# A macaron layer in split float32: the first block's norm and split ahead on VectorE, first loads in a new order, last tokens finished 128 at a time

## The chip, the cores and the metric

The kernel runs on one NeuronCore of a Trainium2 chip. A core has a matrix engine (TensorE, "PE" in the profile), a vector engine (VectorE, "DVE"), a scalar engine for activations and copies (ScalarE, "ACT"), a general engine (GpSimd, "POOL") and a queueing engine (SyncE, "SP"). Each runs its own list of instructions in order; semaphores tie them together. Transfers between main memory (HBM) and the on-chip memory (SBUF) are issued here from the SP queue and from the GpSimd queue; TensorE writes to eight banks of accumulation memory (PSUM).

The metric is the device time of one launch in microseconds (us). A profiled execution also leaves a trace, whose span runs from the first to the last instruction.

## What is computed

The input x has 4 sequences of 1024 positions with 256 features. Three residual steps follow one another:

```python
x = x + 0.5 * ffn(layernorm(x), ...)          # turn "f" in the kernel
x = x + attn(layernorm(x), ...)               # an S4D long convolution, "mix"
x = x + 0.5 * ffn(layernorm(x), ...)          # turn "g", same weights as "f"

def ffn(x, ...):                              # weights are -1, 0, 1; s is a scale per row
    h = silu(x @ w1.T * w1_s) * (x @ w2.T * w2_s)      # 256 -> 1024
    h = gelu(h @ h1.T * h1_s)                          # 1024 -> 1024
    h = gelu(h @ h2.T * h2_s)                          # 1024 -> 1024
    return h @ w3.T * w3_s                             # 1024 -> 256

def attn(x, ...):
    K = s4d_kernel(...)                       # 256 filters of 1024 taps
    y = irfft(rfft(x, 2048) * rfft(K, 2048))[:1024]
    return gelu(y) @ W.T + b
```

Everything is float32.

## The kernel before

The 4096 positions are cut into eight blocks of 512 (`TB`), each four tiles of 128 positions (`JT = 4`). The program goes through 16 turns in order: ("f", 0) to ("f", 7), then ("g", 0) to ("g", 7) (L771). One turn is one call of `ffn` (L247). The convolution of the four sequences (`mix`, L638), the computation of the filter's spectrum (`kernel_steps`, `kernel_spectrum`) and a check of the weights run beside the turns: a generator (`all_aside`, L794) is advanced one step at each `tick()` inside `ffn`.

An activation is kept as a pair: a high part rounded to a shorter float format ("fp32r") and a low part, the remainder (`low_part`, L217). A product with a ternary weight is then two matmuls of 128x128 by 128x512 into the same bank, one for each part (`linear`, L235).

In `ffn` there are eight output tiles m per layer. The gated layer takes 8 matmuls per m, four into `pa` (w1) and four into `pb` (w2): 64 in all. ScalarE makes silu(pa) (L258), VectorE multiplies by pb (L259), ScalarE casts the high part (L261), VectorE makes the low part (L217). Layers 2 and 3 take 16 matmuls per m, 128 per layer; ScalarE's gelu (L271) and cast (L273) and VectorE's remainder (L217) follow each m. The output layer (L289 to L312) works on two token tiles at a time: 32 matmuls of 256 columns into one bank (`po`), VectorE scales by 0.5 and w3_s (L303), GpSimd adds the residual (L311), and SP stores 256 KB (L312). The last call of the last turn ends the kernel, apart from a flag (`bad`, L836) that says whether every weight was held exactly; all engines read it at L844 and would run an unsplit version if it were set.

The input of the next turn is prepared during the current one (`prepare`, L774): its load (`load_x`, L166, three buffers `xb`), its norm (L198: statistics L204, their aggregation L206, the square root on ScalarE L207, then reciprocal L209 and normalisation L211 on VectorE), and its transposes on TensorE with the split of the result (`transposed`, L219). For block 0 the norm and transposes come ahead of the loop (L808 to L810).

The order of work on an engine is not written out: a scheduler orders all instructions by priority and by when it thinks that their operands are ready, and gives out buffers and semaphores. So an instruction of a later block may stand ahead of one of block 0 on the same engine, and once the list is fixed an engine waits at its head.

The first loads, in the order of the program (L178 to L195): SP takes x of block 0, the constants `cst`, the `scales`, x of block 1, the filter's parameters `k_in` (L187, L188), then `w3_s`, `wt` and `bias`; GpSimd's queue takes w1 and w2 in four pieces of 512 KB, h1 and h2 in eight pieces of 1 MB, and w3.

Of the kernel before, what the change touches and what calls it, by code (L numbers as in the profile page):

```python
# [2 lines left out]

# [1 line left out]

# [6 lines left out]
F32 = mybir.dt.float32  # L12
# [79 lines left out]
def macaron_layers(  # L92
# [34 lines left out]
    def bank(name):  # L127
        return psum.tile([P, 512], F32, tag="ps", name=name)
# [5 lines left out]
    def ring(name, *shape, dtype=F32):  # L134

        return work.tile([P, *shape], dtype, tag="ring", name=name, bufs=15)
# [23 lines left out]
    def column(i):  # L160
        return cst_sb[:, i : i + 1]

    def positions(t, b, j, n=2):
        return t[b].rearrange("(p j) d -> p j d", j=J)[:, j : j + n, :]

    def load_x(t, blk, name):  # L166
        b, g = divmod(blk, J // JT)
        xb = work.tile([P, JT, D], F32, tag="xb", name=name, bufs=3)
        nc.sync.dma_start(xb, positions(t, b, g * JT, JT))
        return xb  # L170

    def rows(w):
# [2 lines left out]

    weights_from = nc.gpsimd if split else nc.sync

    x_first = load_x(x, 0, "x_f0")  # L178
    nc.sync.dma_start(cst_sb[:, 0:C_N], cst)
    nc.sync.dma_start(sc_sb, scales)  # L180
    for k in range(DC):
        weights_from.dma_start(w1_sb[:, k, :], rows(w1)[:, k, :])
        weights_from.dma_start(w2_sb[:, k, :], rows(w2)[:, k, :])
    x_second = load_x(x, 1, "x_f1")
    k_in = half("k_in", 4, DD)
    k_in2 = half("k_in2", 4, DD)
    nc.sync.dma_start(k_in, kin[:, 0:4, :])  # L187
    nc.sync.dma_start(k_in2[:, 0, :], kin[:, 4, :])  # L188
    for t, src in ((h1_sb, h1), (h2_sb, h2)):
        for k in range(0, KH, 2):  # L190
            weights_from.dma_start(t[:, k : k + 2, :], rows(src)[:, k : k + 2, :])
# [3 lines left out]
    nc.sync.dma_start(bias_sb, bias.partition_broadcast(P))  # L195


    def norm(t, name):  # L198

        stats = small.tile([P, JT, 6], F32, tag="stats", name=f"stats_{name}")  # L200
        mv = small.tile([P, JT, 2], F32, tag="mv", name=f"mv_{name}")
        rstd = small.tile([P, JT], F32, tag="rstd", name=f"rstd_{name}")
        for i in range(JT):
            nc.vector.bn_stats(stats[:, i, :], t[:, i, :])  # L204
        for i in range(JT):
            nc.vector.bn_aggr(mv[:, i, :], stats[:, i, :])  # L206
        nc.scalar.activation(rstd, mv[:, :, 1], AF.Sqrt, bias=column(C_EPS))  # L207
        yield
        nc.vector.reciprocal(rstd, rstd)  # L209
        for i in range(JT):  # L210
            ts(t[:, i, :], t[:, i, :], mv[:, i, 0:1], rstd[:, i : i + 1], ALU.subtract, ALU.mult)  # L211
        yield


    def low_part(t, src):

        tt(t[:, 1, :], src, t[:, 0, :].bitcast(F32), ALU.subtract)  # L217

    def transposed(xn, name):  # L219

        xt = []
        for k in range(DC):
            pt = bank(f"pt_{name}_{k}")
            for i in range(JT):
                nc.tensor.transpose(  # L225
                    pt[:, i * P : (i + 1) * P], xn[:, i, k * P : (k + 1) * P], ident
                )
            t = ring(f"xt_{name}_{k}", parts, TB, dtype=wide)
            nc.vector.tensor_copy(t[:, 0, :], pt)  # L229
            if split:  # L230
                low_part(t, pt)
            xt.append(t)
        return xt

    def linear(ps, w, m, acts):  # L235
        n = len(acts)
# [7 lines left out]
                    stop=(k == n - 1 and part == parts - 1),  # L244
                )

    def ffn(xt, src, dst, blk, name, tick, ahead):  # L247

        ha = []
        for m in range(KH):
            pa, pb = bank(f"pa_{name}_{m}"), bank(f"pb_{name}_{m}")
            linear(pa, w1_sb, m, xt)
            linear(pb, w2_sb, m, xt)
            g = half(f"g_{name}_{m}")
            t = ring(f"ha_{name}_{m}", parts, TB, dtype=wide)
            nc.scalar.activation(g, pa, AF.Silu, scale=sc_sb[:, 0, m : m + 1])  # L258
            stt(g if split else t[:, 0, :], pb, sc_sb[:, 1, m : m + 1], g, ALU.mult, ALU.mult)  # L259
            if split:  # L260
                nc.scalar.copy(t[:, 0, :], g)  # L261
                low_part(t, g)
            ha.append(t)
        for layer, w in ((2, h1_sb), (3, h2_sb)):
            hb = []
            for m in range(KH):
                ps = bank(f"p{layer}_{name}_{m}")
                linear(ps, w, m, ha)
                t = ring(f"h{layer}_{name}_{m}", parts, TB, dtype=wide)
                g = half(f"g{layer}_{name}_{m}") if split else t[:, 0, :]  # L270
                nc.scalar.activation(g, ps, AF.Gelu, scale=sc_sb[:, layer, m : m + 1])  # L271
                if split:
                    nc.scalar.copy(t[:, 0, :], g)  # L273
                    low_part(t, g)
                hb.append(t)
                if layer == 3:
                    ahead()
                if m < KH - 1:
                    tick()
            ha = hb  # L280
        ahead(last=True)
        tick()
        b, g = divmod(blk, J // JT)
        rest = []
        for i in range(0, JT, 2):
            xr = half(f"xr_{name}_{i}", 2, D)
            nc.sync.dma_start(xr, positions(src, b, g * JT + i))
            rest.append(xr)
        for i in range(0, JT, 2):  # L289
            xr = rest[i // 2]  # L290
            ps = bank(f"po_{name}_{i}")
            for e in range(2):
                for k in range(KH):
                    for part in range(parts):
                        nc.tensor.matmul(  # L295
                            ps[:, e * D : (e + 1) * D],
                            ha[k][:, part, (i + e) * P : (i + e + 1) * P],
                            w3_sb[:, k, :],
                            start=(k == 0 and part == 0),
                            stop=(k == KH - 1 and part == parts - 1),  # L300
                        )
            y = half(f"y_{name}_{i}", 2, D)
            stt(  # L303
                y,
                ps.rearrange("p (e d) -> p e d", e=2),
                0.5,
                w3s_sb[:, None, :].to_broadcast([P, 2, D]),
                ALU.mult,
                ALU.mult,
            )  # L310
            nc.gpsimd.tensor_tensor(y, xr, y, ALU.add)  # L311
            nc.sync.dma_start(positions(dst, b, g * JT + i), y)  # L312

    def weight_checks():

# [489 lines left out]
            yield from weight_checks()  # L805

    aside = all_aside()
    for _ in norm(x_first, "f0"):  # L808
        pass
    xt = transposed(x_first, "f0")  # L810
    for n, (turn, blk) in enumerate(blocks):
        following = []
        steps = [prepare(*b, following) for b in blocks[n + 1 : n + 2]]

        def ahead(last=False):
            for step in steps:
                if last:
                    done.append(("last layer", *blocks[n + 1][::-1]))
                next(step, None)

        src, dst = (x, x1) if turn == "f" else (x2, out)
        ffn(xt, src, dst, blk, f"{turn}{blk}", lambda: next(aside, None), ahead)
        done.append((turn, blk))
        xt = following
    for _ in aside:
# [86 lines left out]
```

## Time and profile before

| | us |
|---|---|
| median of three executions | 1465.45 |
| lowest and highest | 1464.86 and 1466.04 |
| the profiled execution | 1466.05 |
| its span, first to last instruction | 1464.1 |
| VectorE busy in the span | 860.5 |
| ScalarE busy in the span | 666.1 |
| one matmul 128x512, mean of its modelled duration in layers 2 and 3 | 0.39 |
| one silu or gelu of 128x512 (L258, L271) | 0.69 |
| one cast of 128x512 on ScalarE (L273) | 0.62 |
| one remainder of 128x512 on VectorE (L217) | 0.69 |
| one product with the gate on VectorE (L259) | 0.75 |

The profile is read in steps. The page gives each engine's busy time and, in 40 slices, when it is busy. The chain of waits is followed back from the last instruction to whatever released it. The waits name, for an engine that stood idle, which instruction waited and what released it. The timeline lists instructions in order of start. Matmuls are pipelined and their ends are modelled, so their spacing (0.227 us in long rows, the chain's 240 matmuls in 54.42) says more than their duration. Idle time of an engine that isn't the one everything waits for costs nothing.

### The profile page before, as it was taken

To read this page: it belongs to the slowest core of one execution; us is meant where nothing else is said; L and a number is where in the kernel's file an instruction comes from. 1 tells how busy PE (TensorE), PEld (TensorE's weight loads), DVE (VectorE), ACT (ScalarE), POOL (GpSimd) and SP (SyncE) were. 2 spreads that over 40 slices of the span, in tenths; PEclk is the share of its full clock that TensorE was granted. 3 is DMA by queue.
4 is the path that set the end of the run, shared out by engine and by line. 5 is a ranking of instruction groups with operands and counts; after the bars stand their busy time and mean duration, and the time that the engine had idled before them with its cause. 6 is when DMAs were issued, how large, how long until landed. Compare 5 with 4: busy or idle time off the path is not lost.

```text
span 1464.1 us, 18076 instructions
## 1 busy us (share of the span) xinstructions
PE 1429.7 (98%) x7074; PEld 1213.7 (83%) x7074; DVE 860.5 (59%) x1616; ACT 666.1 (45%) x996; POOL 74.4 (5%) x71
## 2 busy tenths in 40 slices
PE   5999999999999999997999999999999999999997
PEld 4788888888888888886888888888888888888886
DVE  5776574765744634667367673676736667464521
ACT  3677353783534434442454344543445334353432
POOL 2000000000000000000100001000010000100000
PEclk9999999999999999999999999999999999999999
DMA  9110000100001111210312113121121111633000
GB/s 365 33 42 2 15 30 4 40 1 29 15 29 44 62 46 38 72 58 29 101 51 87 37 36 94 48 89 37 36 94 44 65 37 36 221 117 101 21 9 17
DMA packets 42975, 85.50 MB, mean 58 GB/s; under 512 B 4737, under 2 KB 9985, under 8 KB 42881
## 3 DMA queue, kind: packets, MB, share of 16 engines
q1 hardware_dynamic: 39088, 72.73, 15.1%
q0 software_dynamic: 3792, 11.54, 2.2%
q8 instruction: 57, 0.93, 0.3%
q14 instruction: 38, 0.30, 0.1%
HBM read 69.05 MB, written 15.20 MB: 58 GB/s over the span
## 4 chain that ended last, share of the span: by engine, by line
PE 94%; DMA 2%; DVE 2%; ACT 1%; issue 0%; POOL 0%; SPq 0%; POOLq 0%; DVEq 0%
PE p_f L239 32%; PE p_g L239 30%; PE po_f L295 4%; PE po_g L295 4%; PE pa_g L239 4%; PE pb_g L239 4%; PE pa_f L239 3%; PE pb_f L239 3%; PE pi L731 2%; PE pf_m L561 2%; PE pk L497 2%; PE pw L751 2%; DMA x_f<-in_x_dram 1%; DMA k_in<-in_kin_dram 1%; PE pt_f L225 1%; DVE given L328 1%
## 5 line engine op out<-in xcount | busy, mean ns | idle before, releaser
L239 PE MATMUL p_f<-ha_f,h_sb 128*128 128x512 f32 x1024 | 242.4, 394 | 1.8 <-ACT ha_f L261 0.9
L239 PE MATMUL p_f<-h_f,h_sb 128*128 128x512 f32 x1024 | 240.4, 392 | 0.0
L239 PE MATMUL p_g<-h_g,h_sb 128*128 128x512 f32 x1024 | 236.0, 390 | 0.0
L239 PE MATMUL p_g<-ha_g,h_sb 128*128 128x512 f32 x1024 | 234.5, 390 | 0.0
L239 PEld LDWEIGHTS p_f<-ha_f,h_sb 128*128 128x128 f32 x1024 | 192.2, 189 | 43.5 <-ACT ha_f L261 1.6
L239 PEld LDWEIGHTS p_g<-ha_g,h_sb 128*128 128x128 f32 x1024 | 192.2, 188 | 39.9
L239 PEld LDWEIGHTS p_g<-h_g,h_sb 128*128 128x128 f32 x1024 | 192.2, 188 | 39.8
L239 PEld LDWEIGHTS p_f<-h_f,h_sb 128*128 128x128 f32 x1024 | 190.9, 188 | 40.0 <-DVE h_f L217 0.3
L271 ACT ACTIVATE g_g<-p_g,sc_sb 128x512 f32<-128x512 f32 x128 | 88.2, 689 | 273.4 <-PE p_g L239 268.6
L217 DVE TENSOR_TENSOR h_f<-g_f,h_f 128x512 fp32r<-128x512 f32 x128 | 88.3, 691 | 193.0 <-ACT h_f L273 192.8
L271 ACT ACTIVATE g_f<-p_f,sc_sb 128x512 f32<-128x512 f32 x128 | 88.0, 688 | 245.6 <-PE p_f L239 245.3
L217 DVE TENSOR_TENSOR h_g<-g_g,h_g 128x512 fp32r<-128x512 f32 x128 | 88.4, 691 | 171.4 <-ACT h_g L273 171.1
L273 ACT CAST h_g<-g_g 128x512 fp32r<-128x512 f32 x128 | 79.4, 620 | 3.9
L273 ACT CAST h_f<-g_f 128x512 fp32r<-128x512 f32 x128 | 79.1, 619 | 3.4
L258 ACT ACTIVATE g_g<-pa_g,sc_sb 128x512 f32<-128x512 f32 x64 | 44.0, 687 | 66.5 <-PE pa_g L239 64.4
L239 PE MATMUL pa_f<-xt_f,w_sb 128*128 128x512 f32 x256 | 70.5, 395 | 1.8 <-DVE xt_f L229 1.2
L259 DVE SCALAR_TENSOR_TENSOR g_g<-pb_g,sc_sb,g_g 128x512 f32<-128x512 f32 x64 | 47.9, 748 | 37.2 <-PE pb_g L239 29.8
L239 PE MATMUL pb_f<-xt_f,w_sb 128*128 128x512 f32 x256 | 69.2, 392 | 0.0
L239 PE MATMUL pa_g<-xt_g,w_sb 128*128 128x512 f32 x256 | 68.6, 390 | 0.0
L239 PE MATMUL pb_g<-xt_g,w_sb 128*128 128x512 f32 x256 | 68.4, 389 | 0.0
L295 PE MATMUL po_g<-w_sb,h_g 128*128 128x256 f32 x512 | 64.2, 285 | 2.2 <-DVE h_g L217 2.2
L295 PEld LDWEIGHTS po_g<-w_sb,h_g 128*128 128x128 f32 x512 | 62.3, 192 | 2.9 <-DVE h_g L217 2.8
(216 smaller groups left out, 1682.3 us busy)
## 6 DMA issues: line engine op xcount, KB each, us to landing
h_sb<-in_h_dram POOLq DMA_DIRECT2D x8, 1024.0 KB, 22.6
given<-in_h_dram SPq DMA_DIRECT2D x32, 256.0 KB, 4.7
kr<-k_hat SPq DMA_DIRECT2D x20, 256.0 KB, 2.7
ki<-k_hat SPq DMA_DIRECT2D x20, 256.0 KB, 2.9
x_f<-in_x_dram SPq DMA_DIRECT2D x8, 512.0 KB, 3.8
xr_f<-in_x_dram SPq DMA_DIRECT2D x16, 256.0 KB, 3.5
x<-y_f SPq DMA_DIRECT2D x16, 256.0 KB, 2.4
xm<-x SPq DMA_DIRECT2D x8, 512.0 KB, 4.1
```

Source lines behind the costliest of these rows:

```text
L217: tt(t[:, 1, :], src, t[:, 0, :].bitcast(F32), ALU.subtract)
L225: nc.tensor.transpose(pt[:, i * P : (i + 1) * P], xn[:, i, k * P : (k + 1) * P], ident)
L239: nc.tensor.matmul(ps, w[:, k, m * P : (m + 1) * P], acts[k][:, part, :], start=(k == 0 and part == 0), stop=(k == n - 1 and part == parts ...
L258: nc.scalar.activation(g, pa, AF.Silu, scale=sc_sb[:, 0, m : m + 1])
L259: stt(g if split else t[:, 0, :], pb, sc_sb[:, 1, m : m + 1], g, ALU.mult, ALU.mult)
L271: nc.scalar.activation(g, ps, AF.Gelu, scale=sc_sb[:, layer, m : m + 1])
L273: nc.scalar.copy(t[:, 0, :], g)
L295: nc.tensor.matmul(ps[:, e * D : (e + 1) * D], ha[k][:, part, (i + e) * P : (i + e + 1) * P], w3_sb[:, k, :], start=(k == 0 and part == 0) ...
L497: nc.tensor.matmul(pk[:, at + i, :, :].rearrange("p h b -> p (h b)"), a[:, i].rearrange("p a b -> p (a b)"), qd[d1 // per_tile][:, at + i, ...
L561: nc.tensor.matmul(ps[e][:, part, :], m[:, e, part, :], rows_of(q + JQ * e), start=True, stop=True)
L731: nc.tensor.matmul(banks[dc][e][:, q * P : (q + 1) * P], vs[q + JQ * e][:, part, dc * P : (dc + 1) * P], m[:, e, part, :], start=(part == ...
L751: nc.tensor.matmul(ps[:, e * D : (e + 1) * D], yts[dc][j // JQ][:, (j % JQ + e) * P : (j % JQ + e + 1) * P], wt_sb[:, dc, :], start=(dc == 0),
```

## The change

Four edits, all in the split version that runs:

- Loads. Block 0's x is loaded as two transfers of two token tiles each. Block 1's x, `k_in` and `k_in2` move from SP's queue to GpSimd's queue, behind w1 and w2 and ahead of h1.
- Norm and transposes of block 0. `norm` takes `parts_of`: for block 0 (`parts_of=2`) statistics, root, reciprocal and normalisation are done for two token tiles at a time. `transposed` takes `first`: the transposes then go token tile by token tile over both banks, VectorE copies the high part of xt_0, ScalarE that of xt_1, and the two remainders follow on VectorE.
- Order. The whole first call of `ffn`, with all that is traced within it (the steps of `all_aside` and the preparation of block 1 among them), stands in a block `tc.issue_after(last_split.ins)`. It puts each VectorE instruction traced in it behind the last remainder of block 0's split on VectorE. It adds no wait of its own at run time; it fixes the order.
- Output. In the last turn (`final`), the last two token tiles get a bank each, 16 matmuls each; for each of them VectorE scales 128x256, VectorE and not GpSimd adds the residual, and SP stores 128 KB.

As the scheduler builds it, TensorE's list is unchanged but for the order of block 0's transposes and first products. VectorE's list begins with block 0's statistics, reciprocals and normalisations, one copy and two remainders; then come three of block 1's four statistics; then the eight gates of block 0 with their remainders and the product on k_in; then the norms of blocks 1, 2 and 3, mixed with the filter's computation and the remainders of layer 2. From about the 127th entry to the end of the last turn VectorE's list is the old one. ScalarE's table switches for the roots of blocks 1 to 3 stand behind block 0's gates instead of among them. On SP, the read of the flag follows the last store; before, it came ahead of it.

```diff
@@ -163,10 +163,10 @@
     def positions(t, b, j, n=2):
         return t[b].rearrange("(p j) d -> p j d", j=J)[:, j : j + n, :]
 
-    def load_x(t, blk, name):
+    def load_x(t, blk, name, queue=nc.sync):
         b, g = divmod(blk, J // JT)
         xb = work.tile([P, JT, D], F32, tag="xb", name=name, bufs=3)
-        nc.sync.dma_start(xb, positions(t, b, g * JT, JT))
+        queue.dma_start(xb, positions(t, b, g * JT, JT))
         return xb
 
     def rows(w):
@@ -175,17 +175,20 @@
 
     weights_from = nc.gpsimd if split else nc.sync
 
-    x_first = load_x(x, 0, "x_f0")
+    x_first = work.tile([P, JT, D], F32, tag="xb", name="x_f0", bufs=3)
+    for i in range(0, JT, 2):
+        nc.sync.dma_start(x_first[:, i : i + 2, :], positions(x, 0, i))
     nc.sync.dma_start(cst_sb[:, 0:C_N], cst)
     nc.sync.dma_start(sc_sb, scales)
     for k in range(DC):
         weights_from.dma_start(w1_sb[:, k, :], rows(w1)[:, k, :])
         weights_from.dma_start(w2_sb[:, k, :], rows(w2)[:, k, :])
-    x_second = load_x(x, 1, "x_f1")
+
+    x_second = load_x(x, 1, "x_f1", queue=weights_from)
     k_in = half("k_in", 4, DD)
     k_in2 = half("k_in2", 4, DD)
-    nc.sync.dma_start(k_in, kin[:, 0:4, :])
-    nc.sync.dma_start(k_in2[:, 0, :], kin[:, 4, :])
+    weights_from.dma_start(k_in, kin[:, 0:4, :])
+    weights_from.dma_start(k_in2[:, 0, :], kin[:, 4, :])
     for t, src in ((h1_sb, h1), (h2_sb, h2)):
         for k in range(0, KH, 2):
             weights_from.dma_start(t[:, k : k + 2, :], rows(src)[:, k : k + 2, :])
@@ -195,42 +198,60 @@
     nc.sync.dma_start(bias_sb, bias.partition_broadcast(P))
 
 
-    def norm(t, name):
+    def norm(t, name, parts_of=1):
 
         stats = small.tile([P, JT, 6], F32, tag="stats", name=f"stats_{name}")
         mv = small.tile([P, JT, 2], F32, tag="mv", name=f"mv_{name}")
         rstd = small.tile([P, JT], F32, tag="rstd", name=f"rstd_{name}")
-        for i in range(JT):
-            nc.vector.bn_stats(stats[:, i, :], t[:, i, :])
-        for i in range(JT):
-            nc.vector.bn_aggr(mv[:, i, :], stats[:, i, :])
-        nc.scalar.activation(rstd, mv[:, :, 1], AF.Sqrt, bias=column(C_EPS))
-        yield
-        nc.vector.reciprocal(rstd, rstd)
-        for i in range(JT):
-            ts(t[:, i, :], t[:, i, :], mv[:, i, 0:1], rstd[:, i : i + 1], ALU.subtract, ALU.mult)
+        step = JT // parts_of
+        for at in range(0, JT, step):
+            here = range(at, at + step)
+            for i in here:
+                nc.vector.bn_stats(stats[:, i, :], t[:, i, :])
+            for i in here:
+                nc.vector.bn_aggr(mv[:, i, :], stats[:, i, :])
+            nc.scalar.activation(
+                rstd[:, at : at + step], mv[:, at : at + step, 1], AF.Sqrt, bias=column(C_EPS)
+            )
+        yield
+        for at in range(0, JT, step):
+            nc.vector.reciprocal(rstd[:, at : at + step], rstd[:, at : at + step])
+            for i in range(at, at + step):
+                ts(
+                    t[:, i, :],
+                    t[:, i, :],
+                    mv[:, i, 0:1],
+                    rstd[:, i : i + 1],
+                    ALU.subtract,
+                    ALU.mult,
+                )
         yield
 
 
     def low_part(t, src):
 
-        tt(t[:, 1, :], src, t[:, 0, :].bitcast(F32), ALU.subtract)
-
-    def transposed(xn, name):
-
-        xt = []
+        return tt(t[:, 1, :], src, t[:, 0, :].bitcast(F32), ALU.subtract)
+
+    def transposed(xn, name, first=False):
+
+
+        pts = [bank(f"pt_{name}_{k}") for k in range(DC)]
+        order = [(k, i) for k in range(DC) for i in range(JT)]
+        for k, i in sorted(order, key=lambda o: o[1]) if first else order:
+            nc.tensor.transpose(
+                pts[k][:, i * P : (i + 1) * P], xn[:, i, k * P : (k + 1) * P], ident
+            )
+        xt = [ring(f"xt_{name}_{k}", parts, TB, dtype=wide) for k in range(DC)]
+        last = None
+        if first:
+            last = nc.vector.tensor_copy(xt[0][:, 0, :], pts[0])
+            nc.scalar.copy(xt[1][:, 0, :], pts[1])
         for k in range(DC):
-            pt = bank(f"pt_{name}_{k}")
-            for i in range(JT):
-                nc.tensor.transpose(
-                    pt[:, i * P : (i + 1) * P], xn[:, i, k * P : (k + 1) * P], ident
-                )
-            t = ring(f"xt_{name}_{k}", parts, TB, dtype=wide)
-            nc.vector.tensor_copy(t[:, 0, :], pt)
+            if not first:
+                nc.vector.tensor_copy(xt[k][:, 0, :], pts[k])
             if split:
-                low_part(t, pt)
-            xt.append(t)
-        return xt
+                last = low_part(xt[k], pts[k])
+        return (xt, last) if first else xt
 
     def linear(ps, w, m, acts):
         n = len(acts)
@@ -244,7 +265,7 @@
                     stop=(k == n - 1 and part == parts - 1),
                 )
 
-    def ffn(xt, src, dst, blk, name, tick, ahead):
+    def ffn(xt, src, dst, blk, name, tick, ahead, final):
 
 
 
@@ -286,10 +307,10 @@
             xr = half(f"xr_{name}_{i}", 2, D)
             nc.sync.dma_start(xr, positions(src, b, g * JT + i))
             rest.append(xr)
-        for i in range(0, JT, 2):
-            xr = rest[i // 2]
-            ps = bank(f"po_{name}_{i}")
-            for e in range(2):
+
+        def result(ps, i, n):
+
+            for e in range(n):
                 for k in range(KH):
                     for part in range(parts):
                         nc.tensor.matmul(
@@ -299,17 +320,37 @@
                             start=(k == 0 and part == 0),
                             stop=(k == KH - 1 and part == parts - 1),
                         )
-            y = half(f"y_{name}_{i}", 2, D)
+
+        def finish(ps, y, xr, i, n, add_on):
             stt(
                 y,
-                ps.rearrange("p (e d) -> p e d", e=2),
+                ps.rearrange("p (e d) -> p e d", e=n),
                 0.5,
-                w3s_sb[:, None, :].to_broadcast([P, 2, D]),
+                w3s_sb[:, None, :].to_broadcast([P, n, D]),
                 ALU.mult,
                 ALU.mult,
             )
-            nc.gpsimd.tensor_tensor(y, xr, y, ALU.add)
-            nc.sync.dma_start(positions(dst, b, g * JT + i), y)
+            add_on.tensor_tensor(y, xr, y, ALU.add)
+            nc.sync.dma_start(positions(dst, b, g * JT + i, n), y)
+
+        for i in range(0, JT, 2):
+            y = half(f"y_{name}_{i}", 2, D)
+            if final and i + 2 == JT:
+                for e in range(2):
+                    ps = bank(f"po_{name}_{i + e}")
+                    result(ps, i + e, 1)
+                    finish(
+                        ps[:, 0:D],
+                        y[:, e : e + 1, :],
+                        rest[i // 2][:, e : e + 1, :],
+                        i + e,
+                        1,
+                        nc.vector,
+                    )
+            else:
+                ps = bank(f"po_{name}_{i}")
+                result(ps, i, 2)
+                finish(ps, y, rest[i // 2], i, 2, nc.gpsimd)
 
     def weight_checks():
 
@@ -805,9 +846,9 @@
             yield from weight_checks()
 
     aside = all_aside()
-    for _ in norm(x_first, "f0"):
+    for _ in norm(x_first, "f0", parts_of=2):
         pass
-    xt = transposed(x_first, "f0")
+    xt, last_split = transposed(x_first, "f0", first=True)
     for n, (turn, blk) in enumerate(blocks):
         following = []
         steps = [prepare(*b, following) for b in blocks[n + 1 : n + 2]]
@@ -819,7 +860,8 @@
                 next(step, None)
 
         src, dst = (x, x1) if turn == "f" else (x2, out)
-        ffn(xt, src, dst, blk, f"{turn}{blk}", lambda: next(aside, None), ahead)
+        with tc.issue_after(last_split.ins) if n == 0 else nullcontext():
+            ffn(xt, src, dst, blk, f"{turn}{blk}", lambda: next(aside, None), ahead, n + 1 == len(blocks))
         done.append((turn, blk))
         xt = following
     for _ in aside:
```

More of the change, by code (lines that the diff above doesn't have):

```diff
@@ L1 @@
 import math
-from contextlib import ExitStack
+from contextlib import ExitStack, nullcontext
 import numpy as np
```

## The prediction

> **What bounds the kernel now.** I read the page first. TensorE is busy in 98% of the span, and in its 40 slices only the first and last, and two in the middle, are not full:
>
> ```profile
> PE 1429.7 (98%) x7074; PEld 1213.7 (83%) x7074; DVE 860.5 (59%) x1616; ACT 666.1 (45%) x996; POOL 74.4 (5%) x71
> PE   5999999999999999997999999999999999999997
> ```
>
> So a change can only gain where TensorE stands still. The waits of TensorE over the whole run say where that is; nearly all of it is the start and one place near 690 us:
>
> ```profile
> PE pt_f L225 <- DVE x_f L211: 13.8, 1, 13.8
> PE pi L731 <- DVE v_False L722: 7.4, 1, 7.4
> ```
>
> The change touches the first and leaves the second. The timeline of the first microseconds (start, duration, engine, line, operation, idle time before it and what ended it):
>
> ```profile
> 4.51 1.41 DVE L204 BATCH_NORM_STATS2 stats_f<-x_f 128x6 f32<-128x256 f32 x4 [3.63 <-DMA x_f<-in_x_dram]
> 4.74 1.28 ACT L207 ACT_TABLE_LOAD   x1 [4.74 <-DMA cst_sb<-in_cst_dram]
> 6.23 0.30 ACT L207 ACTIVATE rstd_f<-mv_f,cst_sb 128x4 f32<-128x4 f32 x1 [0.21 <-DVE mv_f L206]
> 10.89 1.08 DVE L204 BATCH_NORM_STATS2 stats_f<-x_f 128x6 f32<-128x256 f32 x3 [4.70 <-DMA x_f<-in_x_dram]
> 11.89 0.16 DVE L209 RECIPROCAL rstd_f<-rstd_f 128x4 f32<-128x4 f32 x1
> 12.96 0.29 DVE L413 TENSOR_SCALAR k_in<-k_in,cst_sb 128x128 f32<-128x128 f32 x1 [0.91 <-DMA k_in<-in_kin_dram]
> 13.16 1.46 DVE L211 TENSOR_SCALAR x_f<-x_f,mv_f,rstd_f 128x256 f32<-128x256 f32 x4
> 13.76 2.24 PE L225 MATMUL pt_f<-ident,x_f 128*128 128x128 f32 x8 [13.76 <-DVE x_f L211]
> 17.21 1.72 PE L239 MATMUL pa_f<-xt_f,w_sb 128*128 128x512 f32 x2 [1.20 <-DVE xt_f L229]
> 23.95 1.41 DVE L204 BATCH_NORM_STATS2 stats_f<-x_f 128x6 f32<-128x256 f32 x4 [4.36 <-DMA x_f<-in_x_dram]
> 38.96 0.50 PE L239 MATMUL p_f<-ha_f,h_sb 128*128 128x512 f32 x1 [0.22 <-DVE ha_f L217]
> ```
>
> Block 0's 1/std is ready at 6.53, but VectorE runs in order and the queue's next entries are block 1's statistics (their load lands at 10.89) and a product on k_in (lands about 12.9). So 1/std waits till 11.89 and the normalisation till 13.16. Later VectorE waits at 23.95 and 26.56 for the statistics of blocks 2 and 3, and ScalarE swaps tables for their roots, all while block 0's gates stand behind; TensorE starves between 35 and 40.35. Its clock then drops (stretches of time: busy PE, PEld, DVE, ACT, POOL; granted clock, DMA share, GB/s):
>
> ```profile
> 42.00:43.00 1.00, 1.00 (x4) 0.81 (x3) 0.97 (x4) 0.12 (x1) 0.00 (x0) 0.50 0.00 0
> 47.00:48.00 1.00, 1.00 (x7) 0.81 (x6) 0.00 (x0) 0.97 (x2) 0.00 (x0) 1.00 0.00 0
> ```
>
> The end: last products, then VectorE's scaling, GpSimd's addition, the store:
>
> ```profile
> 1448.41 8.09 PE L295 MATMUL po_g<-w_sb,h_g 128*128 128x256 f32 x64
> 1456.54 0.69 DVE L303 SCALAR_TENSOR_TENSOR y_g<-po_g,w3s_sb 128x512 f32<-128x512 f32 x1 [2.78 <-PE po_g L295]
> 1457.36 1.26 POOL L311 TENSOR_TENSOR y_g<-xr_g,y_g 128x512 f32<-128x512 f32 x1 [2.18 <-DVE bad L836]
> 1455.21 3.79 SPq L312 DMA_DIRECT2D out_dram<-y_g  x2
> ```
>
> [...] matmuls start 0.43 us apart from 18.72, and 0.227 us apart only after 21.0, 3.8 us after the first; the clock is 0.50 from 41.25 to 44.5. [...] against 4 KB packets of weights on GpSimd's queue, SP's 1 KB packets crawl (wt takes 14.9 us, bias 15.4), so block 2's load, issued at 6.62 behind them, lands at 23.95.
>
> **The change part by part.** Zero is the start of the profiled span.
>
> Block 0's norm. The load becomes two of 256 KB; cst is now third on SP, not second, one issue of 0.41 us later. ScalarE's table load waits for cst: 4.74 + 0.41 = 5.15, loaded at 6.4, first root (0.30) at 6.7. The statistics and aggregations, 1.41 + 0.36 = 1.8 us, fit before that unless a half lands after about 4.9, so the split load gains little: the table is the limit. Then two reciprocals (0.16) and four normalisations (0.35 apart), with gaps, 6.75 to 8.6. Transposes now go token tile by token tile, the last pair starts at 8.65 and ends at 9.3 (0.26 apart). Cast of xt_0 0.68: first matmul at 10.0 instead of 17.21. xt_1 is copied by ScalarE meanwhile (a 128x512 copy from PSUM takes 0.59 at L565), so the two remainders, 0.68 each, are done at 10.6 and 11.2; TensorE's first xt_1 product is its tenth. Bound: a half or cst landing 0.7 later moves all this by 0.7; earlier by at most 0.4, since only cst's extra issue was added.
>
> Weights. GpSimd's next issues show the four pieces of w1 and w2 landed by 8.27, 10.84, 12.87 and 14.48. The new order needs them at matmul 1, 2, 10 and 17: 10.0, 10.4, about 14.3 and 16. Even at the old landings only 0.4 is lost. SP now has one 512 KB load fewer before them, which makes them earlier; I take 0, range 0 to 0.8.
>
> Gates of block 0 (64 matmuls). Half rate at first: [...] I take 4.5, to 14.5, with 10 matmuls done. The other 54 take 0.2268 each (the chain has 240 in 54.42): 12.2, so they end at 26.7. VectorE: 8 x (0.75 + 0.69) = 11.5 us, ScalarE 8 x (0.69 + 0.62) = 10.5 us, both less than TensorE, as the built order puts only three statistics of block 1 ahead of the gates and the rest of blocks 1 to 3 behind. Block 1's load moves to GpSimd's queue, fifth, behind 2 MB of w1 and w2, and should land at 13 to 17. VectorE waits there with all gates behind it. The first gate then is ready 1.8 us later (three statistics, one 0.75), and TensorE needs its bank at matmul 41, at 21.3: a landing up to 19.5 costs nothing. The last remainder comes at about 29.7 even then; the built order reaches it as the 23rd matmul of the next layer, at 31.5.
>
> h1. Its first 1 MB landed by 17.7; x_f1 and k_in (0.84 MB) now go ahead: 2.1 us at 400 GB/s, so 19.8, then 2.6 us per MB to 27.7. Needed from 26.7, the last quarter after 20 matmuls, 31.2. No stall; margin 3 us.
>
> Layers 2 and 3. Before, TensorE reaches block 1's transposes at 97.41; 256 products at 0.2268 are 58.1, so full rate would have begun at 39.35. After: 26.7. Gain 12.65: 7.2 in the first matmul, 5.45 in stalls and the 1.7 us of half clock [...]. The moved norms (about 9 us of VectorE) land in block 0's layers 2 and 3, where VectorE has room: 59% over the run. From about VectorE's 127th entry all engines' orders match the old, and TensorE has no wait till 684.7, so the gain is carried through.
>
> End. Two banks, two halves. Scaling and addition of 128x256 take 0.42 each on VectorE (L703 shows that shape): 1456.43 + 0.11 + 0.42 + 0.05 + 0.42 = 1457.43, against 1458.62: gain 1.2. SP now reads the flag behind the last store instead of ahead of it: 0 to 0.8 lost; a store of half the size lands 0 to 0.3 sooner. I take 1.2, range 0.4 to 1.5.
>
> Sum: 12.65 + 1.2 = 13.85. The profiled execution took 1466.05 (span 1464.1 and 1.95 around it), so 1452.2; it is 0.6 above the median of 1465.45, so against that 1451.6.
>
> **The rivals.**
> Loads or a cold array hold the start: one of the late cases above each (cst or a half 0.7, weights 0.8, [...] h1 or bank waits 2), 4.6 together: 1456.2. For it: DMA is saturated until 40. Against: bytes ahead of w1, w2 shrank.
> Given back at 690: if VectorE's later work were a backlog, the 7.4 us wait at L731 grows by 12.65, and only the end gains: 1464.3, no measurable change. Against: VectorE last waited for ScalarE's cast at 686.14, which follows TensorE, so that wait is a local chain of about 5 us.
> Slower: block 1's load heads VectorE's queue ahead of every gate. If GpSimd's queue doesn't serve in order and x_f1 lands with the last loads, at about 39.5, TensorE stalls 39.5 - 19.5 = 20: 1471.6. It decides from a landing at 19.5 + 13.85 = 33.4. For it: x_f2 took 17.3 us from issue. Against: w1 and w2 landed in their order in 14.5 us.
> That the change fails to do what it says is excluded by the built order: block 0's norm is first on VectorE.
>
> **How the numbers follow.** Forecast 0.76; held start 0.15; given back 0.04; slower 0.03; and 0.02 for a start better by 3 (warm at once, weights and x early): 1448.6. The forecast's own spread is 1449.5 to 1454.5; with the held start, 1449.2 to 1456.5 holds 8 in 10 and somewhat more. This kernel's measurement tells 0.2%, 2.9 us, from no change. Faster 0.93, same 0.04, slower 0.03.
>
> **What would show it.** First matmul near 10 with block 0's reciprocal before any other block's statistics; no wait of TensorE for ha_f; block 1's transposes at 84.8; no half clock near 42; the L731 wait still near 7.4; VectorE's last addition about 1.0 us after the last matmul. Wrong would be: x_f1 landing after 19.5, TensorE waiting for w_sb or h_sb, or a second half-clock stretch in block 0.

## The result, and the profile after

| | before | after |
|---|---|---|
| median of six executions, us | 1465.38 | 1455.69 |
| lowest and highest | 1464.86 and 1466.04 | 1454.43 and 1457.52 |
| ratio to before, with its 95% interval | | 0.9936 [0.9923, 0.9948] |
| the profiled execution, and its span | 1466.05, 1464.1 | 1457.52, 1455.7 |

The change gains 9.7 us. The forecast of 1451.6 is 4.1 too low; the stated range, 1449.2 to 1456.5, holds the result. Where the time went is read from the timeline of the changed kernel's start (start, duration, engine, line, operation, idle time before it and what ended it):

```profile
3.97 0.75 DVE L210 BATCH_NORM_STATS2 stats_f<-x_f 128x6 f32<-128x256 f32 x2 [3.10 <-DMA x_f<-in_x_dram]
...
5.29 0.75 DVE L210 BATCH_NORM_STATS2 stats_f<-x_f 128x6 f32<-128x256 f32 x2 [0.36 <-DMA x_f<-in_x_dram]
...
7.67 1.28 ACT L213 ACT_TABLE_LOAD   x1 [7.67 <-DMA cst_sb<-in_cst_dram]
...
9.29 0.17 DVE L218 RECIPROCAL rstd_f<-rstd_f 128x2 f32<-128x2 f32 x1 [3.03 <-ACT rstd_f L213]
...
12.64 0.80 PE L260 MATMUL pa_f<-xt_f,w_sb 128*128 128x512 f32 x1 [0.57 <-DVE xt_f L247]
...
14.00 1.08 DVE L210 BATCH_NORM_STATS2 stats_f<-x_f 128x6 f32<-128x256 f32 x3
```

Block 0's first half of x lands at 3.97 and its second at 5.29, and VectorE has no other block's work in front. Everything then waits for ScalarE's table, which waits for `cst`: 7.67. Block 1's statistics come at 14.00, without a wait. The waits of TensorE over the whole run (total, times, longest):

```profile
PE pt_f L241 <- DVE x_f L220: 10.1, 1, 10.1
PE pi L772 <- DVE v_False L763: 7.4, 1, 7.4
```

There is no wait for ha_f any more, the wait at 690 us is 7.4 as before, and the one at the start is 3.7 shorter. Four marks in the two traces split the span: first matmul of 128x512, first transpose of block 1, last product of the output layer (where the small matmul for the flag starts), end.

| stretch, us | before | after | gain | predicted gain |
|---|---|---|---|---|
| to the first matmul | 17.21 | 12.64 | 4.57 | 7.2 |
| from there to block 1's transposes | 80.20 | 74.76 | 5.44 | 5.4 |
| from there to the last product | 1359.02 | 1360.92 | -1.90 | 0 |
| from there to the end | 7.67 | 7.38 | 0.29 | 1.2 |
| span | 1464.1 | 1455.7 | 8.4 | 13.85 |

The third row is lost at one place, near 1280 us in the changed kernel, where TensorE waits in both kernels for remainders of h_g. The products behind the last of these waits, before:

```profile
1288.76 6.14 PE L295 MATMUL po_g<-w_sb,h_g 128*128 128x256 f32 x49 [1.31 <-DVE h_g L217]
```

And after, with one microsecond of their time (stretch, its length, busy PE, PEld, DVE, ACT, POOL; granted clock, DMA share, GB/s):

```profile
1279.17 7.61 PE L316 MATMUL po_g<-w_sb,h_g 128*128 128x256 f32 x49 [1.31 <-DVE h_g L233]
...
1280.00:1281.00 1.00, 1.00 (x7) 1.00 (x6) 1.00 (x4) 0.00 (x0) 0.00 (x0) 0.51 0.00 0
```

The same 49 products take 7.61 us instead of 6.14, as the clock is half for 3.4 us: 1.5 of the 1.9. A first, shorter wait just before, 1.15 us after and 0.85 before, adds 0.3. The drop does not belong to the change: `own_eps` and `own_eps_again` below are one kernel, and from block 1's transposes to the last product the first trace needs 1358.14 us without the drop, the second 1360.74 with it. Which of the other five executions of the changed kernel had it is not known. Two of the six, the profiled one among them, show a mean clock of 0.995 and took 1457.5 and 1457.2; four show 0.997 and took 1454.4 to 1455.8. That would fit, but the mean alone does not prove it: `old_tail` shows 0.995 without this drop, with a half-clock stretch of 10.2 us near 680 where the changed kernel's has 6.8.

### The profile page after: what moved, and what is told of

Its sections match the earlier page's. It is cut to its first block, busy times and chain, and to the rows that moved or that the text cites. A ratio compares the mean times of both kernels' runs of the same rounds, so it can differ in the third digit from the quotient of the medians.

```text
span 1455.7 us, 18086 instructions
## 1 busy us (share of the span) xinstructions
PE 1427.9 (98%) x7074; PEld 1214.5 (83%) x7074; DVE 860.2 (59%) x1619; ACT 664.7 (46%) x996; POOL 74.7 (5%) x73
## 4 chain that ended last, share of the span: by engine, by line
PE 96%; DVE 2%; DMA 1%; issue 0%; ACT 0%; POOL 0%; SPq 0%; POOLq 0%; ACTq 0%
PE p_f L260 32%; PE p_g L260 30%; PE po_f L316 4%; PE po_g L316 4%; PE pa_f L260 4%; PE pb_f L260 4%; PE pa_g L260 4%; PE pb_g L260 4%; PE pi L772 2%; PE pf_m L602 2%; PE pk L538 2%; PE pw L792 2%; DVE given L369 1%; PE pt_f L241 1%; PE pf_k L602 0%; DMA x_g<-x 0%
```

## The experiments

The runs fall into three sets, each on one chip with runs of the kernel before beside it. Ratios are to those, with 95% intervals; times are medians. The changed kernel was timed in a set of its own, so a difference to it is one of ratios from different sets, and differences of 1 or 2 us rest on the traces more than on the times.

### Where the start is held: cst, its place, or the table

`cst_first` moves one line: `cst` goes ahead of x on SP.

```diff
+    nc.sync.dma_start(cst_sb[:, 0:C_N], cst)
     x_first = work.tile([P, JT, D], F32, tag="xb", name="x_f0", bufs=3)
     for i in range(0, JT, 2):
         nc.sync.dma_start(x_first[:, i : i + 2, :], positions(x, 0, i))
-    nc.sync.dma_start(cst_sb[:, 0:C_N], cst)
```

> The changed kernel with the constants cst as SP's first load, ahead of the two halves of block 0's x; every engine's list of computing instructions is the same. Table theory (the first root waits for ScalarE's table load, which waits for cst, landed at 7.67 in the changed kernel): cst lands by 4, the table is in by 5.3, the first root comes when the statistics do, about 5.5 to 6.5, and the first 128x512 matmul starts at 9.5 to 10.3 instead of 12.64; block 1's transposes near 85 instead of 87.4; 2.3 to 2.8 us faster than the changed kernel. Rival (what is put first on SP only delays the rest): the second half of x lands at 6.5 or later instead of 5.29, the first matmul at 11 or later, and the gain is under 1.5 us.

`own_eps` leaves the loads alone and takes the table's wait for `cst` away: the root's bias comes from a column of its own, filled on VectorE.

```diff
+    eps_sb = keep.tile([P, 1], F32, name="eps_sb")
+    nc.vector.memset(eps_sb, EPS)
...
-                rstd[:, at : at + step], mv[:, at : at + step, 1], AF.Sqrt, bias=column(C_EPS)
+                rstd[:, at : at + step], mv[:, at : at + step, 1], AF.Sqrt, bias=eps_sb
```

> The changed kernel with the root's epsilon in a tile that VectorE fills, so that no instruction of block 0's norm needs cst; the loads stand as in the changed kernel. Table theory: ScalarE's table load runs in the first 3 us, x still lands at 3.97 and 5.29, the first matmul starts at 9.4 to 10.2, 2.5 to 3.2 us faster than the changed kernel. Rival (VectorE or the x loads set the start): the first matmul moves by less than 1 us.

Measured: `cst_first` 1453.76, ratio 0.9928 [0.9915, 0.9942]; `own_eps` 1452.07, ratio 0.9918 [0.9904, 0.9931]. The timeline of `cst_first`:

```profile
2.52 1.28 ACT L213 ACT_TABLE_LOAD   x1 [2.52 <-DMA cst_sb<-in_cst_dram]
...
7.14 0.75 DVE L210 BATCH_NORM_STATS2 stats_f<-x_f 128x6 f32<-128x256 f32 x2 [1.18 <-DMA x_f<-in_x_dram]
...
11.22 0.80 PE L260 MATMUL pa_f<-xt_f,w_sb 128*128 128x512 f32 x1 [0.57 <-DVE xt_f L247]
```

And of `own_eps`:

```profile
0.74 1.28 ACT L215 ACT_TABLE_LOAD   x1 [0.74 <-PEq L942]
...
5.38 0.75 DVE L212 BATCH_NORM_STATS2 stats_f<-x_f 128x6 f32<-128x256 f32 x2
...
9.46 0.80 PE L262 MATMUL pa_f<-xt_f,w_sb 128*128 128x512 f32 x1 [0.57 <-DVE xt_f L249]
```

With `cst` first, the table is loaded at 3.8, but the second half of x is now SP's third transfer, and it lands at 7.14: the first matmul moves from 12.64 to 11.22 only, as its rival expected. Without the need for `cst`, the table is loaded at 2.0, both halves have landed by 5.38, and the first matmul is at 9.46. The table's wait held the start, by 3.2 us. (The intervals of `own_eps` and of the changed kernel, 0.9923 to 0.9948, overlap; the later run `own_eps_again` repeats the trace.)

`x_whole` asks whether `cst` was late through its place on SP or through the larger load of GpSimd's queue. It loads block 0's x in one transfer, so `cst` is second again, and all else is as in the changed kernel.

```diff
-    x_first = work.tile([P, JT, D], F32, tag="xb", name="x_f0", bufs=3)
-    for i in range(0, JT, 2):
-        nc.sync.dma_start(x_first[:, i : i + 2, :], positions(x, 0, i))
+    x_first = load_x(x, 0, "x_f0")
```

> Block 0's x in one transfer, so the constants are second on SyncE's queue as before. Theory (whichever transfer is third on SyncE lands at 7 to 8): constants near 4.7, first root near 6.5, first matmul 9.6 to 10.3, 2.3 to 3 us below after, ratio 0.991 to 0.9925; the scales land near 8. Rival (the constants are slow since GpSimd's queue now holds 0.84 MB more behind the weights): constants still at 7 or later, first matmul above 12, ratio 0.9936.

Measured: 1453.96, ratio 0.9919 [0.9906, 0.9931]. The timeline of `x_whole`:

```profile
4.98 1.28 ACT L211 ACT_TABLE_LOAD   x1 [4.98 <-DMA cst_sb<-in_cst_dram]
...
9.83 0.80 PE L258 MATMUL pa_f<-xt_f,w_sb 128*128 128x512 f32 x1 [0.57 <-DVE xt_f L245]
```

`cst` lands at 4.98 and the first matmul starts at 9.83. So the place on SP decides, not the bytes on GpSimd's queue: the split of x pushes `cst` into the slow place. Halving x's load, part of the change, thus costs 2.8 us at the first matmul (12.64 against 9.83). (`old_loads` and `loads_no_order` below agree: GpSimd's queue is the old one there, and `cst`, third on SP, lands at 8.11 and 7.73.) What remains open is what makes it slow. The third transfer is issued at 1.67, the second at 1.20, and GpSimd's first weights at 1.28; a limit by count and a collision with the weights would look the same here.

The norm in two parts and the new order of the transposes were not run by themselves. At the first matmul they show no gain: from the landing of `cst` to it the old norm takes 4.78 us (`order_only` below, 4.74 to 9.52), the new one 4.85 in `x_whole` and 4.97 in the changed kernel.

### Which part carries the gain: the loads or the order

`old_loads` puts x_f1, k_in and k_in2 back on SP and keeps all else; `loads_no_order` does that and also leaves out the order block; `order_only` is the kernel before with the order block alone. A version of the changed kernel without the order block was not run, since the scheduler builds it into the same instructions, in the same order, on every engine. Which of the moved loads matters, x_f1 or k_in, was not separated.

```diff
-    x_second = load_x(x, 1, "x_f1", queue=weights_from)
+    x_second = load_x(x, 1, "x_f1")
...
-    weights_from.dma_start(k_in, kin[:, 0:4, :])
-    weights_from.dma_start(k_in2[:, 0, :], kin[:, 4, :])
+    nc.sync.dma_start(k_in, kin[:, 0:4, :])
+    nc.sync.dma_start(k_in2[:, 0, :], kin[:, 4, :])
```

> The changed kernel with block 1's x and k_in back on SP's queue in their old place; halves of x, norm in parts and the order block stay. In its list VectorE still does block 0's norm and split first, but k_in's product, all statistics of blocks 1 and 2 and two of block 3 stand ahead of block 0's first gate. Theory (the queue of these loads sets the list, and the list sets the stalls): the first matmul stays at 11.5 to 13.5, the first gate comes only when block 3's x has landed, at 22 or later instead of 19.2, TensorE waits among the gates again, 2 to 6 us slower than the changed kernel. Rival (the order block alone keeps the gain): within 0.7 us of the changed kernel.

And, on top of that:

```diff
-        with tc.issue_after(last_split.ins) if n == 0 else nullcontext():
-            ffn(xt, src, dst, blk, f"{turn}{blk}", lambda: next(aside, None), ahead, n + 1 == len(blocks))
+        ffn(xt, src, dst, blk, f"{turn}{blk}", lambda: next(aside, None), ahead, n + 1 == len(blocks))
```

> As the last, and without the order block. In its list two of block 0's four normalisations stand behind a statistic of block 1, and block 0's split stands behind the whole norm of block 1, the product on k_in and a statistic of block 2. Theory: the first matmul waits for block 2's x, 20 us or later, TensorE starves about as in the kernel before: 1463 to 1469 us. Rival (the halves and the interleaved transposes make the gain by themselves): first matmul under 15 and within 2 us of the changed kernel.

The edit of `order_only`, on the kernel before (where `transposed` also returns its last remainder):

```diff
-        ffn(xt, src, dst, blk, f"{turn}{blk}", lambda: next(aside, None), ahead)
+        with tc.issue_after(last_split.ins) if n == 0 and split else nullcontext():
+            ffn(xt, src, dst, blk, f"{turn}{blk}", lambda: next(aside, None), ahead)
```

> The kernel before with the order block alone: the first call of ffn is traced behind the last remainder of block 0's split. The loads, the norm in one part, cst as SP's second load stay as before. Theory: cst lands at 4.7 as before, so block 0's root at 6.5 is used at once and the first matmul starts at 9.8 to 10.8, earlier than in the changed kernel (12.64); but statistics of blocks 1 to 3 still stand ahead of the gates, so the first gate waits to 24 or later and TensorE starves there: 2 to 6 us faster than before, 1459 to 1463. Rival (the early norm is all that counts): 1453 to 1455.

| | time | ratio [interval] | first matmul | first gate on VectorE | block 1's transposes |
|---|---|---|---|---|---|
| new loads and order (after) | 1455.69 | 0.9936 [0.9923, 0.9948] | 12.64 | 19.21 | 87.40 |
| `old_loads`, with the order | 1464.72 | 0.9998 [0.9990, 1.0006] | 13.20 | 28.23 | 95.97 |
| `loads_no_order` | 1470.17 | 1.0030 [1.0018, 1.0042] | 25.90 | 32.12 | 100.55 |
| `order_only` | 1462.85 | 0.9985 [0.9976, 0.9994] | 9.52 | 26.10 | 93.31 |

The timeline of `old_loads` shows why an early first matmul is not enough:

```profile
24.84 1.41 DVE L209 BATCH_NORM_STATS2 stats_f<-x_f 128x6 f32<-128x256 f32 x4 [8.59 <-DMA x_f<-in_x_dram]
...
29.02 2.08 PE L259 MATMUL pa_f<-xt_f,w_sb 128*128 128x512 f32 x4 [4.65 <-DVE g_f L279]
```

Its order block put block 0's split first, but with x_f1 on SP the scheduler still set the statistics of blocks 2 and 3 ahead of the first gate. VectorE stood 8.59 us for x_f2 and, later, 1.04 for x_f3, and TensorE stood 4.65 for g_f, the gate that frees its next bank. During that wait its clock falls to half, from 27.3 to 34.2; one microsecond of it, when TensorE works again (columns as for 1280 above):

```profile
33.00:34.00 1.00, 1.00 (x4) 0.77 (x3) 1.00 (x4) 0.99 (x2) 0.00 (x0) 0.50 1.09 410
```

From 29.02 on TensorE works at half clock for 5.1 us, which loses another 2.6 (an estimate, half of 5.1). The expectation of 2 to 6 us did not price this; by the ratios `old_loads` loses the whole gain. A wait of TensorE in `order_only` tells the same of the kernel before:

```profile
PE pa_f L239 <- DVE g_f L259: 6.7, 1, 6.7
```

Its first matmul is even earlier than the changed kernel's (`cst` is second there), but the wait for g_f, and a clock of 0.50 from 22.2 to 32.5, turn a lead of 3.1 us over it into 5.9 behind at block 1's transposes. Without the order block, the timeline of `loads_no_order`:

```profile
24.83 0.43 DVE L209 BATCH_NORM_STATS2 stats_f<-x_f 128x6 f32<-128x256 f32 x1 [7.89 <-DMA x_f<-in_x_dram]
25.18 0.67 DVE L246 CAST xt_f<-pt_f 128x512 fp32r<-128x512 f32 x1
...
25.90 0.80 PE L259 MATMUL pa_f<-xt_f,w_sb 128*128 128x512 f32 x1 [12.51 <-DVE xt_f L246]
```

Here even the cast of xt_0 stands behind a statistic of x_f2, so the new norm and tail without the loads and the order make the kernel slower (1470.17, a little above the 1463 to 1469 expected). The nine microseconds hang on VectorE's list, and the list follows from where the loads are issued: moving x_f1 and k_in to GpSimd's queue keeps later blocks' statistics behind the gates, and then the order block has nothing left to do.

### What ends the kernel: the flag and its jump

The last addition, now VectorE's, ends 0.99 us after the last product, where GpSimd's ended 2.19 us after it: 1.2 sooner, as predicted. But the end moved by 0.29 only. At the end each engine reads the flag (`TENSOR_LOAD` below), jumps over the unsplit version and comes to a closing barrier; the last to come ends the kernel. Instructions of the kernel before (engine, operation, duration in ns three times, first and last start in us):

```profile
L844 SPq TENSOR_LOAD <-bad x1: 471/471/471, 1457.3 to 1457.3; - x1
...
L845 SPq COMPARE_BRANCH  x1: 45/45/45, 1459.0 to 1459.0; - x1
...
L908 SPq DRAIN  x3: 7/7/7, 1463.2 to 1463.6; - x3
...
L908 PEldq DRAIN  x2: 8/8/8, 1462.2 to 1463.6; - x2
```

The same of the changed kernel:

```profile
L886 SPq TENSOR_LOAD <-bad x1: 521/521/521, 1449.7 to 1449.7; - x1
...
L887 SPq EVENT_SEMAPHORE  x8: 17/17/17, 1453.4 to 1454.0; - x8
...
L887 PEldq COMPARE_BRANCH  x1: 4342/4342/4342, 1449.5 to 1449.5; - x1
...
L887 SPq COMPARE_BRANCH  x1: 45/45/45, 1450.6 to 1450.6; - x1
...
L950 POOLq EVENT_SEMAPHORE  x4: 17/17/17, 1454.9 to 1455.6; - x4
...
L950 SPq DRAIN  x3: 7/7/7, 1454.8 to 1455.1; - x3
...
L950 PEldq DRAIN  x2: 8/8/8, 1454.1 to 1455.2; - x2
```

TensorE's jump is the longest, 4.34 us, but it isn't what ends the kernel. TensorE is at the barrier (its first DRAIN) at 1454.1; SP comes last, at 1454.8, and GpSimd opens the barrier at 1454.9. Between its branch and 1454.8 no wait of SP for another engine is recorded: the branch is at 1450.6, SP goes on 2.8 us later, and its closing steps follow about 0.1 us apart. In the kernel before SP comes last too, at 1463.2, and TensorE at 1462.2.

So SP's branch sets the end. It comes 2.6 us after the last product before and 2.3 after: the 0.3 that was gained. SP issues the last store 1.2 us sooner after the last product, since the addition is sooner; but it now reads the flag behind that store and not ahead of it, and from the store's issue to the branch it takes 1.3 us instead of 0.4. That reading costs 0.9 of the 1.2.

The branch instructions themselves say little about this: SP's and GpSimd's are recorded with 45 ns and TensorE's with 4.34 us. From its branch GpSimd takes 0.5 us to go on (1449.5 to 1450.0), SP 2.8 and TensorE 4.3. What sets these times was not shown.

`old_tail` undoes the last edit (the last argument of `ffn` is False); `early_flag` keeps it and moves the flag's sum, matmul and read ahead of the last turn's products.

```diff
+        if split and n + 1 == len(blocks):
+            for _ in aside:
+                pass
...
+            nc.tensor.matmul(ps, total, ones, start=True, stop=True)
+            nc.vector.tensor_copy(bad, ps)
+            n_bad = nc.values_load(bad, min_val=0, max_val=1 << 24)
         with tc.issue_after(last_split.ins) if n == 0 else nullcontext():
```

> The changed kernel without its output edit: the last two token tiles in one bank, scaled together, added by GpSimd, stored as 256 KB. Store theory (as predicted): the end is the last store's chain, so this costs 1.2 us. Flag theory: the end is TensorE's branch on the flag (4.0 to 4.3 us from the flag's reading), which the edit moved by at most 0.3, so from the last matmul's end to the span's end stays within 7.3 to 7.8 us (7.38 in the changed kernel, 7.67 in the kernel before) and the time changes by 0 to 0.4.

> The changed kernel with the flag computed (its sum, its one matmul and its cast) ahead of the last turn instead of at the end. Flag theory: TensorE reads the flag and branches 0.6 us or more sooner after its last matmul, SP does not read it behind the last store; from the last matmul's end to the span's end 6.2 to 6.8 us instead of 7.38, so 0.6 to 1.2 us faster. Store theory: the end follows the last store, which stays where it is, and the time does not change.

Measured: `old_tail` 1456.65, ratio 0.9947 [0.9933, 0.9961], with 8.07 us from the last product to the end; `early_flag` 1454.29, ratio 0.9930 [0.9917, 0.9944], with 6.38 us, where the changed kernel has 7.38. Both intervals overlap the changed kernel's. The 8.07 lies above what the flag theory expected and below what the store theory did. In `old_tail` SP's branch comes 2.6 us after the last product, as in the kernel before, so 0.3 of the 0.7 us is the edit; the rest lies behind the branch, 5.4 us to the end instead of 5.05 in this execution. The flag's line in `early_flag`:

```profile
L891 PEldq COMPARE_BRANCH  x1: 3842/3842/3842, 1444.4 to 1444.4; - x1
L891 SPq COMPARE_BRANCH  x1: 45/45/45, 1447.4 to 1447.4; - x1
```

TensorE's jump now starts at 1444.4, 1.6 us ahead of the last product's end at 1446.0. SP has no flag to read behind the last store, and its branch comes 1.4 us after the last product instead of 2.3: 0.9 of the 1.0 us gained. `no_branch` takes the read and the jump away; it leaves out the unsplit version.

```diff
-        n_bad = nc.values_load(bad, min_val=0, max_val=1 << 24)
-        with tc.If(n_bad > 0):
-            macaron_layers(tc, None, *args)
```

> Leaves out the read of the flag and the unsplit version that it would start. If the jump over that version sets the end (TensorE 4.3 us, SyncE 2.8 us), the stretch from the last product to the end falls from 7.4 to between 3.5 and 4.8 us: the last store's landing of some 2 us and the closing steps of 1.7 remain, so 2.6 to 3.9 us below after. Rival (the last store or the closing steps set the end, the branch only lies beside them): within 0.7 us of after's 7.4.

Measured: 1451.65, ratio 0.9905 [0.9891, 0.9919]; from the last product to the end 4.14 us, 3.2 less. The read and the jump set the end; the last store and the closing steps are the 4.1 beneath them. This run takes away the jumps of all engines at once; that SP's is the one that counts is read from the traces above.

### Both mends together

`eps_flag` is `own_eps` and `early_flag` in one kernel. It ran twice, and `own_eps` was run beside it the second time.

> The changed kernel with both mends: the epsilon in a tile of its own and the flag computed ahead of the last turn. If the two act in separate places, their gains add: first matmul at 9.3 to 9.8, 6.2 to 6.6 us from the last matmul's end to the span's end, 1450.3 to 1451.5 us. Rival (the flag's earlier work costs time in the last turns): no faster than with the epsilon alone, 1452.

> The same kernel as own_eps, beside the next two. Table theory: first matmul 9.4 to 9.6 again, block 1's transposes near 84, ratio 0.991 to 0.9925. Rival (the earlier gain was an accident of that chip): first matmul back at 12 or later, ratio 0.9936 as after.

> Own epsilon column and flag read ahead of the last products. Both parts add: first matmul near 9.5, 6.4 us from the last product to the end, 0.9 to 1.1 us below own_eps on the same chip. Rival (SyncE's own branch behind the last store holds the end, whatever TensorE does): within 0.3 us of own_eps.

| | time | ratio [interval] | first matmul | last product to end |
|---|---|---|---|---|
| `eps_flag` | 1452.19 | 0.9910 [0.9897, 0.9922] | 9.43 | 6.46 |
| `own_eps_again` | 1452.57 | 0.9909 [0.9896, 0.9923] | 9.41 | 7.5 |
| `eps_flag_again` | 1450.29 | 0.9897 [0.9884, 0.9910] | 9.36 | 6.4 |

The first run of `eps_flag` is above the 1450.3 to 1451.5 expected, and by its time alone not faster than `own_eps`. The traces show both parts, 3.2 us at the start and 1.1 at the end. Of the 2.3 us between the last two medians 1.1 are explained by the end, and their intervals overlap; the profiled run of `own_eps_again` also had the half clock near 1280. The intervals of both runs of `eps_flag` lie below the changed kernel's, 0.9923 to 0.9948, so it beats both kernels. That it beats `own_eps` too is shown by the end of the traces, not by the times.

## Why the prediction was right, and where it was off

- Mechanism: right. Block 0's reciprocal comes first, no TensorE wait for ha_f, no half clock near 42 (1.00 from 41 to 45, where the trace of before has 0.50 to 0.72), block 1's load in time, the 7.4 us wait at 690 carried through. From the first matmul to block 1's transposes 74.76 us against 74.8 predicted. That this is so close is in part luck: traces of kernels with the same order of work show 74.3 (`own_eps`) to 75.8 (`x_whole`), as the spacing of the matmuls falls from 0.43 to 0.23 us 3.5 us (`own_eps`) to 6.4 us (`x_whole`) after the first; in the changed kernel's trace it took 4.4. The 4.5 assumed was the author's estimate; the trace of before has 3.8.
- The result lies above the forecast's own spread, 1449.5 to 1454.5. It is in the range because the rival of a held start, given 0.15, had widened it; that rival had the place, with a price of 0.7. What its 4.6 holds for a longer time at half rate was the author's estimate; the longest measured, 6.4, would cost 0.95 against the 4.5 assumed (half the difference). The load of the DMA engines that speaks for this rival is in the trace of before: a share of 0.99 or more, at 333 to 430 GB/s, from 6 to 39 us.
- "one issue of 0.41 us later. ScalarE's table load waits for cst: 4.74 + 0.41 = 5.15": this term failed. `cst` landed at 7.67. From the table's end to the first matmul it took 3.69 us, 3.6 predicted, so that came at 12.64 and not at 10.0: 2.6 of the 5.4 us that the span is off. "the split load gains little" was right in that the table is the limit, but the split is what delayed the table.
- "I take 1.2" at the end: the sum for the additions came true, 1.2 us sooner. The step that failed is the next term, SP's reading of the flag behind the last store, "0 to 0.8 lost", taken at 0. It cost 0.9, so the end gained 0.29: 0.9 of the 5.4.
- The middle was taken to be carried through unchanged: 1.9 was lost there in the profiled execution, 1.5 of it to the half clock near 1280. Against the medians this counts for less: four of the six executions are at 1454.4 to 1455.8.
- A misreading on which nothing rests: in the page's 40 slices one in the middle, not two, is not full.
- "Given back at 690" and "slower by x_f1" did not come. x_f1 was there by 14.00 (13 to 17 predicted, 19.5 the limit).
- Left open by the prediction: which edit sets VectorE's list. It is the loads: once they are moved, the scheduler builds the same list without the order block, and without them the block keeps only the first matmul early. Also left open: that SP's packets are slow beside GpSimd's for their size. The trace of before shows the sizes, 1 KB and 4 KB, and the times (wt 14.9 us, bias 15.4), but no run varied the size.

## What to carry to other kernels

Follow a small constant to what it gates: here a table load waited for a column of epsilon, behind two halves of x, and a memset of that column was worth 3.2 us. Where a scheduler makes the lists, moving a load to another queue is also an edit of the order, and an early start is lost again if the next engine's list has a later block's work in front. At the end of a kernel, look at the lines of the flag, branch and closing instructions too, since the chain of waits may stop at the last arithmetic. Ask there which engine comes to the closing barrier last, not whose instruction is the longest: here a queue's small read behind its last store ate 0.9 of 1.2 us.

## What was not expected of the hardware

- SP's third transfer landed at 7.0 to 8.3 us whichever it was: `cst` at 7.67 (issued at 1.67) in the changed kernel, 7.36 in `no_branch`, 8.11 in `old_loads`, the second half of x at 7.14 in `cst_first`, the scales at 7.04 in `order_only` and 8.3 in `x_whole`. The second landed sooner: `cst` at 4.74 in `order_only` and 4.98 in `x_whole`, the second half of x at 5.46 in `old_loads`.
- The jump over the unsplit version took TensorE 3.84 us (`early_flag`) to 4.50 us (`loads_no_order`) and SP 2.8 us (changed kernel) to 3.0 us (`old_tail`), though SP's branch itself is recorded with 45 ns.
- Waits of TensorE near 1280 were followed by 3.4 us at half clock in some executions and not in others: with it in the changed kernel, which waits 1.15 and 1.31 us there with 0.5 us of work between (clock 0.51 from 1280 to 1281), without it in `x_whole`, where TensorE is idle for 2.36 us from 1250 to 1300 (clock 1.00). Between the first full rate and the last product, the half-clock stretches read are one, two or three times 3.4 us long: 3.4 near 42 in the kernel before and near 1280 in the changed one, 6.8 near 690 in the kernel before, 10.2 near 680 in `x_whole` and `old_tail`. What sets these lengths was not shown.
